# Layer 0 of a four-layer graph network: where the first scores stand in VectorE's queue

## The chip, the cores and the metric

The kernel runs on one core of a Trainium2 chip. The metric is the device time of one launch in microseconds (us), the median of several runs. Before the change it is 1615.28 us (three runs, 1614.99 to 1616.41).

The five engines each have a queue of their own and take it in order: TensorE (PE in the profile; PEld is its weight load), VectorE (DVE), ScalarE (ACT), GpSimd (POOL) and SyncE (SP). SP issues most of the loads, ACT the stores, and POOL the gathers by index. An engine whose next instruction waits for a semaphore does nothing of what stands behind it.

## The reference

Four graph-attention layers run one after the other on `x` (4096 rows of 256 numbers), all with the same 0/1 matrix `adj` (4096 x 4096). `adj` is sparse: a row has a few neighbours and itself. Layer 0 is the one that the change touches:

```
h = maximum(layernorm(x), 0) @ W.T                 # 8 heads of 32
e_l, e_r = sums of h * a_l and h * a_r per head
logits = leaky_relu(e_l[i] + e_r[j], 0.2) + gate * sum_f |curv[i,f] - curv[j,f]| * Wc[h,f]
attn = softmax over the j with adj[i,j] > 0
x = x + sum_j attn[i,j] * h[j]
```

The layers 1, 2 and 3 have other scores, and the same pattern of neighbours.

## The kernel before, in words

The kernel never forms the 4096 x 4096 scores. It finds for each tile of 128 rows the list of columns that hold an edge, gathers the rows of those columns from a table in device memory, and works on the gathered rows. There are 32 tiles (`NT`), numbered t; nine gathers (`EC`) of 128 rows each serve one tile. The gathered rows of a tile are its buffer `g`, of which there are six (`G = 6`).

Layer 0 does two jobs at once. **Finding**: `piece` loads `adj` in 128 pieces of 512 KB through SP and turns each into a mask (on ACT, a few on VectorE); `pack` multiplies the masks on TensorE into keys; sixteen pieces make the keys of one group of four tiles. `rank` takes the largest keys of a tile on VectorE (three MAX8 and two MATCH_REPLACE8), `columns` turns the keys of a group into column numbers (some thirty small VectorE instructions), `places` works out where each edge goes (four matmuls with `degree`, then some eighteen VectorE instructions, the last of which, line 1415, writes `both`), `mark` makes the 0/1 matrix `st` of a tile, and `find_edges` multiplies it on TensorE and ends in line 1466, which writes `nbr`, the indices of the tile's nine gathers. **Attending**: `begin0` and `begin0_late` issue the nine gathers of a tile on POOL and a load of its own rows on SP (line 927), `before0` makes `pb` and `s_f` on TensorE and ACT, `score0` forms `d` (line 1505) and `e` (1507, 1508) from `g` and `pb` on VectorE, `turn_d` and `curve` take `d` through TensorE (1512, 1518), `weigh0` scales the gathered rows (1531, the longest VectorE instruction of the layer), `attend0` sums them on TensorE (934 to 943), `finish0`, `turn1` and `rows1` add the result to `x` and make the row of layer 1's table. `attend0` of a tile frees its `g`, which the gathers of the tile six later need.

The order is set in two ways. `put(when, f, ...)` gives every step of every tile a planned time; the steps are traced in the order of these times. TensorE's queue keeps that order exactly. The other queues are ordered by a scheduler that takes the traced order as priority and puts an instruction where its model of the machine has the inputs ready. `found[t]` is the planned time at which a tile's list is known, `begun[t]` the planned time of its gathers, `w` the time from which the steps after them are counted: `before0` at w - 10, `score0` at w - 9, `turn_d` at w - 7.8, `curve` at w + 2, `weigh0` at w + 3, `attend0` at w + 15. With this problem's sizes `begun[t]` is 91 + 11.5 t, so `w` is 113 + 11.5 t, and the group that holds the tiles 4 to 7 is ranked at 92.5 to 100, has `columns` at 101, `places` at 119 and its first `find_edges` at 127.

`tc.issue_after(i)` is a block: an instruction traced in it stands behind instruction i in the queue of i's engine. It is an order and not a semaphore. Layer 1 and 2 use it already: `scores` (line 1760) goes behind what the dictionary `behind` holds.

Of the kernel before, what the change touches and what calls it, by code (L numbers as in the profile page):

```python
# [21 lines left out]
C = 256  # L22
KC = C // P
H0, D0, CF = 8, 32, 6
# [672 lines left out]
EC = 9  # L697
# [16 lines left out]
def gnn_lists(  # L714
# [27 lines left out]
    nc = tc.nc  # L742
# [88 lines left out]
    behind = {}  # L831
# [23 lines left out]
    def bank(pool, name, dtype=F32):  # L855
        t = pool.tile([P, 512], F32, name=name)
        return t if dtype == F32 else t.bitcast(dtype)
# [96 lines left out]
    with tc.tile_pool(name="keep", bufs=1) as keep, tc.tile_pool(  # L954
# [9 lines left out]
        g = g_pool.tile([P, EC + 1, ROW0], F32, name="g").rearrange("p c k -> p (c k)")  # L964
# [44 lines left out]
        for i, size in enumerate((0.5, 1.0)):  # L1009
            d = keep.tile([P, P], BF16, name=f"off_diag{i}")  # L1010
# [218 lines left out]
        def rank(t):  # L1229

            r, i = divmod(t, RG // P)
            src = bank(ps_t, "pt")[:, : NH * KP]
            for h in range(NH):
                nc.tensor.transpose(
                    src[:, h * KP : (h + 1) * KP], key_t[r, h][:KP, i * P : (i + 1) * P], ident[:KP, :KP]
                )
            left = find.tile([P, NH * KP], F32, name="left", bufs=1)
            for a in range(0, KMAX, 8):
                best = keys[:, t, a : a + 8]
                nc.vector.max(out=best, in_=src)  # L1240
                if a + 8 < KMAX:
                    nc.vector.match_replace(out=left, in_to_replace=best, in_values=src, imm_value=-1.0)
                    src = left
# [65 lines left out]
        lists = {}  # L1309
# [54 lines left out]
        def places(q, n):  # L1364


            s = slice(q, q + n)
            K = KMAX + KX
            is_, lasts, both = lists.pop(q)
            ps = bank(ps_t, "pt")[:, : 4 * n].rearrange("p (a t) -> p a t", a=4)  # L1370
            nc.tensor.matmul(ps[:, 0, :], lhsT=below, rhs=degree[:, s, 0], start=True, stop=True)
            nc.tensor.matmul(ps[:, 1, :], lhsT=up_to, rhs=degree[:, s, 1], start=True, stop=True)
            for i in range(2):
                nc.tensor.matmul(ps[:, 2 + i, :], lhsT=ones, rhs=degree[:, s, i], start=True, stop=True)

            def tmp(name, *shape):
                return find.tile([P, GT, *shape], F32, name=name, bufs=1)[:, :n]


            end, first, step = tmp("end"), tmp("first", 2), tmp("step", 2)  # L1380
            nc.vector.tensor_scalar(end, ps[:, 3, :], -1.0, float(HALF), op0=OP.mult, op1=OP.add)
            nc.vector.tensor_scalar(
                end, end, float(LATE * P - HALF), second, op0=OP.min, op1=OP.mult
            )
            nc.vector.scalar_tensor_tensor(
                at[:, s], ps[:, 0, :], room, end, op0=OP.add, op1=OP.add
            )
            nc.vector.tensor_scalar(at_late[:, s], ps[:, 1, :], float(HALF), None, op0=OP.add)
            nc.scalar.copy(of_tile[:, s, :], ps[:, 2:, :].rearrange("p a t -> p t a"))
            for i, a in enumerate((at, at_late)):  # L1390
                nc.vector.scalar_tensor_tensor(
                    minus[:, s, i], a[:, s], -2.0, degree[:, s, i], op0=OP.mult, op1=OP.subtract
                )


            nc.vector.tensor_sub(first[:, :, 0], at[:, s], lasts[:, :, 1])
            nc.vector.tensor_sub(step[:, :, 0], at_late[:, s], first[:, :, 0])
            nc.vector.tensor_sub(step[:, :, 1], lasts[:, :, 0], degree[:, s, 1])
            nc.vector.tensor_add(first[:, :, 1], at[:, s], step[:, :, 1])
            nc.vector.tensor_sub(step[:, :, 1], at_late[:, s], first[:, :, 1])  # L1400
            nc.vector.tensor_add(step[:, :, 1], step[:, :, 1], lasts[:, :, 1])
            place_, late = tmp("place_", K), is_[:, :, 1, :]
            for i, (a, b) in enumerate(((0, KMAX), (KMAX, K))):
                shape = [P, n, b - a]
                nc.vector.tensor_tensor(
                    late[:, :, a:b], late[:, :, a:b], step[:, :, i : i + 1].to_broadcast(shape),
                    op=OP.mult,
                )
                nc.vector.tensor_tensor(
                    place_[:, :, a:b], first[:, :, i : i + 1].to_broadcast(shape),  # L1410
                    slot[:, None, a:b].to_broadcast(shape), op=OP.add,
                )
            nc.vector.tensor_add(place_, place_, late)

            nc.vector.scalar_tensor_tensor(
                both[:, :, 0, :], is_[:, :, 0, :], float(FAR), place_, op0=OP.mult, op1=OP.add
            )
            for i in range(n):
                of0[q + i]["list"] = both[:, i]

        def fits():

            every = slice(0, NT)

            def tmp(name):
                return find.tile([P, NT], F32, name=name, bufs=1)

            fails(every, keys[:, :, KMAX - 1], 0.0)
            fails(every, more[:, :, 7], 0.0)
            fails(every, at, from_, OP.is_lt)  # L1430
            fails(every, at_late, floor, OP.is_lt)
            end, over, any_ = tmp("end_"), tmp("over"), tmp("any_")
            nc.vector.tensor_add(end, at, degree[:, :, 0])
            fails(every, end, to)
            fails(every, of_tile[:, :, 0], float(LATE * P))
            nc.vector.tensor_add(over, of_tile[:, :, 0], of_tile[:, :, 1])
            fails(every, over, float(EC * P))
            nc.vector.tensor_add(any_, degree[:, :, 0], degree[:, :, 1])
            nc.vector.tensor_add(any_, any_, loop)
            fails(every, any_, 0.5, OP.is_lt)  # L1440
# [60 lines left out]
        def score0(t):  # L1501
            g = of0[t]["g"]
            pe = of0[t]["b"][:, : (EC + 1) * V0].rearrange("p (c k) -> p c k", c=EC + 1)
            d = of0[t]["d"] = work.tile([P, EC, CF], F32, name="d")
            nc.vector.tensor_sub(d, g[:, :EC, C + H0 :], pe[:, :EC, H0:])  # L1505
            e = of0[t]["e"] = work.tile([P, EC + 1, H0], F32, name="e")
            nc.vector.tensor_add(e, g[:, :, C : C + H0], pe[:, :, :H0])
            nc.vector.scalar_tensor_tensor(e, e, 0.2, e, op0=OP.mult, op1=OP.max)
# [58 lines left out]
        def put(when, f, *a):  # L1567
            plan.append((when, len(plan), f, a))
# [5 lines left out]
        def at_piece(i):  # L1574
            return 8 + T_PIECE * min(i, FIRST) + T_LATER * max(i - FIRST, 0)
# [15 lines left out]
        for q, n in groups:  # L1591
            for t in range(q, q + n):
                last = at_piece((t // (RG // P) + 1) * per_r - 1) + 7 + 2.5 * (t % (RG // P))
                put(last, rank, t)
            put(last + 1, columns, q, n)
            put(last + 19, places, q, n)
            for t in range(q, q + n):
                found[t] = last + 23
        first = 17 + NE // P * T_ROWS
        begun = {}  # L1600
# [3 lines left out]
            put(when, mark, t)  # L1604
            put(when + 4, find_edges, t)
        for t in range(NT):
            w = begun[t] + 22
            put(begun[t], begin0, t)
            put(max(begun[t] + 0.1, begun[0] + 12), begin0_late, t)
            put(w - 10, before0, t)  # L1610
            put(w - 9 + 0, score0, t)
            put(w - 7.8 + 0, turn_d, t)
            put(w + 2, curve, t)
            put(w + 3, weigh0, t)
            put(w + 15, attend0, t)
            put(w + 20, finish0, t)
            put(w + 24.6, turn1, t)
            put(w + 27, rows1, t)
        put(found[NT - 1] + 20, fits)
        for _, _, f, a in sorted(plan, key=lambda p: p[:2]):  # L1620
            f(*a)
        bad_1 = const.tile([P, 1], F32, name="bad_1")
        nc.vector.tensor_reduce(bad_1, bad, AX.X, OP.add)

# [489 lines left out]
def gnn_kernel(tc: tile.TileContext, a: dict, out: bass.AP):  # L2114

    nc = tc.nc
    with tc.tile_pool(name="result", bufs=1, space=DRAM) as result:
        misfit = result.tile([1, 1], I32, name="misfit")
        gnn_lists(
            tc, *(a[k] for k in LISTS_TAKE), out, misfit,  # L2120
        )
        flag = nc.values_load(misfit[0:1, 0:1], min_val=0, max_val=1 << 20, skip_runtime_bounds_check_because="a count of rows")
        with tc.If(flag > 0):
            gnn_dense(tc, *(a[k] for k in DENSE_TAKE), out)
# [70 lines left out]
```

## Time and profile before

One profiled execution took 2274.1 us, with a span of 2272.3 us from its first to its last instruction; the median of the runs without a profile is 1615.28 us.

| stretch of the span, us | what runs | PE busy | DVE busy | ACT busy | POOL busy | granted TensorE clock | DMA share |
|---|---|---|---|---|---|---|---|
| 0 to 108 | finding, table of layer 0 | 66.6 | 65.8 | 59.1 | 16.3 | 0.94 | 0.88 |
| 108 to 440 | finding and attending | 161.6 | 154.8 | 139.9 | 137.6 | 0.63 | 0.58 |
| 440 to 780 | the same; the last pieces of `adj` | 208.7 | 168.6 | 121.2 | 137.4 | 0.69 | 0.45 |
| 780 to 860 | from layer 0 to layer 1 | 31.6 | 26.7 | 21.1 | 45.6 | 0.66 | 0.52 |
| 860 to 1340 | layer 1 | 281.4 | 180.6 | 103.6 | 234.7 | 0.74 | 0.46 |
| 1340 to 1850 | layer 2 | 375.3 | 233.3 | 160.0 | 284.8 | 0.86 | 0.51 |
| 1850 to 2272 | layer 3 | 306.0 | 270.5 | 160.3 | 197.8 | 0.88 | 0.41 |

Busy times are us within the stretch. No engine fills a stretch, so what sets the pace is a chain of waits, and the table alone doesn't name it. POOL's busy time is nearly all gathers, 1088 of them in the four layers (288, 256, 288 and 256).

### The profile page before, as it was taken

The numbers are of one execution on the slowest core, as the hardware profiler recorded it, in microseconds if no ns is written. First come the engines' busy times: TensorE is split into PE (matmuls) and PEld (weight loads), VectorE is DVE, ScalarE is ACT, GpSimd is POOL, SyncE is SP. The second block draws the span as 40 slices with busy tenths as digits, with TensorE's granted clock in tenths as the row PEclk, the third lists the DMA queues.
The fourth block names the chain that finished last, engine by engine and source line by source line (L and its number), as shares of the span: only waits on it lengthen the run. The fifth ranks groups of instructions, "written<-read, shape, count | busy, mean of one in ns | idle before, by whom it ended". The sixth has DMA issues, their size and how long they took to land.

```text
span 2272.3 us, 28902 instructions
## 1 busy us (share of the span) xinstructions
PE 1431.2 (63%) x9569; PEld 1013.5 (45%) x9584; DVE 1100.3 (48%) x2979; ACT 765.2 (34%) x2246; POOL 1054.0 (46%) x1145
## 2 busy tenths in 40 slices
PE   5723745656646726656556637878889367767776
PEld 3412423333434414434444425666667345445544
DVE  5724635555543524434333323554555256666666
ACT  4623624454222322222222102333334143343343
POOL 2154243443344354454444455666562635565550
PEclk9855766666666857777777858999999778898888
DMA  8855555665333354444444444555554444455530
GB/s 284 267 187 172 187 172 180 212 212 163 83 88 99 88 164 130 128 124 129 130 133 131 140 138 122 158 161 157 155 156 139 129 134 147 149 157 154 161 107 21
DMA packets 167341, 338.02 MB, mean 149 GB/s; under 512 B 31760, under 2 KB 103696, under 8 KB 167184
## 3 DMA queue, kind: packets, MB, share of 16 engines
q0 software_dynamic: 52224, 145.30, 24.5%
q1 hardware_dynamic: 67714, 134.54, 18.1%
q10 hardware_dynamic: 47246, 56.27, 7.1%
q8 instruction: 77, 1.26, 0.2%
q14 instruction: 80, 0.66, 0.1%
HBM read 282.22 MB, written 53.77 MB: 148 GB/s over the span
## 4 chain that ended last, share of the span: by engine, by line
PE 25%; issue 12%; DVE 9%; another core or an unknown queue 8%; ACT 3%; POOL 1%; DMA 1%; DVEq 0%; ACTq 0%; POOLq 0%
PE o L934 5%; PE o L1894 4%; PE o L939 4%; PE pv L2025 3%; PE pt L872 3%; DVE v L2031 2%; PE pt L1929 2%; PE o L943 1%; POOL g L914 1%; DVE s L2052 1%; PE s_ps L1641 1%; DMA g<-table,nbr 1%; PE pe L1674 1%; DVE g L2064 1%
## 5 line engine op out<-in xcount | busy, mean ns | idle before, releaser
L914 POOL DMA_INDIRECT g<-table,nbr x1088 | 1037.8, 954 | 1065.1 <-issue 433.9
L1894 PE MATMUL o<-g,sw 128*128 128x257 f32 x896 | 206.0, 388 | 31.2 <-DVE sw L1872 23.6
L1894 PEld LDWEIGHTS o<-g,sw 128*128 128x128 f32 x896 | 173.1, 194 | 59.7 <-issue 25.3
L863 PE MATMUL pt<-ident,r 128*128 128x128 f32 x256 | 61.9, 328 | 193.4 <-DVE r L843 60.4
L2025 PE MATMUL pv<-parts,st 64*128 64x256 bf16 (+1 forms) x864 | 106.3, 308 | 97.8 <-DVE v L2031 42.0
L2031 DVE TENSOR_TENSOR v<-pv,g 128x512 f32<-128x512 f32 (+1 forms) x160 | 97.3, 634 | 89.6 <-remote 51.2
L863 PEld LDWEIGHTS pt<-ident,r 128*128 128x128 f32 x256 | 34.4, 162 | 219.2 <-issue 115.4
L1192 ACT ACTIVATE mask<-adj,minus_half 128x1024 bf16<-128x1024 int32 x112 | 125.2, 1141 | 18.1 <-issue 6.8
L934 PE MATMUL o<-g,sw 128*128 128x257 f32 (+1 forms) x320 | 125.5, 544 | 0.0
L865 ACT COPY hT<-pt 128x256 f32<-128x256 f32 x128 | 46.9, 367 | 233.4 <-PE pt L863 144.3
L872 PE MATMUL pt<-wcat,hT 128*128 128x272 f32 (+2 forms) x384 | 96.7, 371 | 45.3 <-ACT hT L865 32.4
L1674 PE MATMUL pe<-ident,col_late 128*128 128x128 f32 x64 | 23.3, 463 | 158.2 <-issue 144.8
L2025 PEld LDWEIGHTS <-st 64*128 64x128 bf16 (+1 forms) x864 | 61.4, 104 | 136.6 <-issue 125.9
L2081 ACT ACTIVATE y<-o,inv 128x64 f32<-128x64 f32 x128 | 36.0, 312 | 243.4 <-DVE inv L2077 143.5
L939 PE MATMUL o<-g,sw 128*64 128x257 f32 (+1 forms) x768 | 117.3, 448 | 0.0
L896 ACT ACTIVATE off<-place,minus 128x1152 bf16<-128x1152 f16 x64 | 80.0, 1250 | 58.1 <-DVE st L897 53.0
L1505 DVE TENSOR_TENSOR d<-g,pb 128x54 f32<-128x54 f32 x32 | 6.8, 211 | 180.1 <-remote 124.9
L934 PEld LDWEIGHTS o<-g,sw 128*128 128x128 f32 x320 | 85.8, 279 | 18.1 <-DVE g L2064 0.3
L872 PEld LDWEIGHTS pt<-wcat,hT 128*128 128x128 f32 x384 | 66.1, 208 | 60.2 <-ACT hT L865 36.5
L1531 DVE TENSOR_TENSOR g<-g,pb 128x2560 f32<-128x2560 f32 x32 | 90.1, 2816 | 4.7 <-ACT pb L1528 4.4
L1674 PEld LDWEIGHTS pe<-ident,col_late 128*128 128x128 f32 x64 | 14.7, 285 | 168.3 <-issue 153.1
L1688 PEld LDWEIGHTS <-st 128*128 128x128 bf16 x768 | 76.7, 105 | 19.4 <-issue 8.6
(363 smaller groups left out, 3028.5 us busy)
## 6 DMA issues: line engine op xcount, KB each, us to landing
adj<-in_adj_l SPq DMA_DIRECT2D x128, 512.0 KB
g<-table,nbr POOLq DMA_INDIRECT x1088
rows_of<-st ACTq DMA_DIRECT2D x16, 832.0 KB
st<-rows_of SPq DMA_DIRECT2D x16, 832.0 KB
x<-x SPq DMA_DIRECT2D x24, 512.0 KB
st<-rows_of SPq DMA_DIRECT2D x16, 576.0 KB
table<-row ACTq DMA_DIRECT2D x32, 258.0 KB
g<-table SPq DMA_DIRECT2D x64, 129.0 KB
```

What stands on the lines that cost most here:

```text
L863: nc.tensor.transpose(pt[:, k, :], h[:, k * P : (k + 1) * P], ident)
L872: nc.tensor.matmul(pp, lhsT=hT[:, k, :], rhs=w[:, k, :], start=(k == 0), stop=(k == KC - 1))
L896: nc.scalar.activation(off, place, AF.Abs, bias=minus[:, t, 0:1], scale=1.0)
L914: nc.gpsimd.indirect_dma_start(out=g[:, c, :width], out_offset=None, in_=table[: NE if c < EARLY else N, :], in_offset=bass.IndirectOffset ...
L934: nc.tensor.matmul(o, lhsT=a, rhs=b, start=(i == 0), stop=False)
L939: nc.tensor.matmul(o[rows], lhsT=s[:, c + h * HC, rows], rhs=g[:, c + h * HC, :width], start=False, stop=False,)
L1192: nc.scalar.activation(m, a, AF.Sign, bias=minus_half, scale=1.0)
L1531: nc.vector.tensor_mul(gh, gh, w[:, :, :, None].to_broadcast([P, K, H0, D0]))
L1688: nc.tensor.matmul(ps, lhsT=to[:, b * P : (b + 1) * P], rhs=late_rows[:, b, i, :width], start=(b == 0 and i == 0), stop=(b == LB - 1 and i ...
L1894: nc.tensor.matmul(o, lhsT=sw[:, h, i].rearrange("p s r -> p (s r)"), rhs=g[:, c, : C + 1], start=(i == 0), stop=(i == HC + 1),)
L2025: nc.tensor.matmul(to, lhsT=st[r, c * P : (c + 1) * P], rhs=parts[r, i, :], start=(i == 0), stop=(i == 2),)
L2031: nc.vector.tensor_mul(v[:, chunks, :], pv, g[:, chunks, :C])
```

## The change

`behind["lists"]` keeps the newest instruction of the finding that was traced: the MAX8 of `rank`, or the last instruction of `places`. In the first two tiles of every group of four, the first instruction of `score0`, the subtraction that writes `d`, is traced in a block behind that instruction. The bound `t < 32` holds for every tile. The two other instructions of `score0` get no order of their own. `w` becomes the larger of its old value and 121 + 8 t, which differs for the tiles 0, 1 and 2 alone: 121, 129 and 137 in place of 113, 124.5 and 136. Since every step from `before0` to `rows1` is counted from `w`, these steps of the three tiles are traced later by 8, 4.5 and 1 planned us; the gathers are not. At the end of layer 0 the entry is taken out of `behind`, so that `scores` of the layers 1 and 2 doesn't see it.

```
-                nc.vector.max(out=best, in_=src)
+                behind["lists"] = nc.vector.max(out=best, in_=src)
...
-            nc.vector.scalar_tensor_tensor(
+            last = nc.vector.scalar_tensor_tensor(
                 both[:, :, 0, :], is_[:, :, 0, :], float(FAR), place_, op0=OP.mult, op1=OP.add
             )
             for i in range(n):
                 of0[q + i]["list"] = both[:, i]
+            behind["lists"] = last
...
-            nc.vector.tensor_sub(d, g[:, :EC, C + H0 :], pe[:, :EC, H0:])
+            with ExitStack() as queue:
+                if t < 32 and t % 4 < 2:
+                    queue.enter_context(tc.issue_after(behind["lists"].ins))
+                nc.vector.tensor_sub(d, g[:, :EC, C + H0 :], pe[:, :EC, H0:])
...
-            w = begun[t] + 22
+            w = max(begun[t] + 22, begun[0] + 30 + 8 * t)
...
         for _, _, f, a in sorted(plan, key=lambda p: p[:2]):
             f(*a)
+        behind.pop("lists")
```

No computation is added or removed.

## The prediction

> **What bounds the kernel now.** I read five views in this order: the page's costliest groups, the timeline of POOL, the view of line 1505, the timeline of VectorE around it, and the waits of TensorE.
>
> ```profile
> L914 POOL DMA_INDIRECT g<-table,nbr x1088 | 1037.8, 954 | 1065.1 <-issue 433.9
> L1505 DVE TENSOR_TENSOR d<-g,pb 128x54 f32<-128x54 f32 x32 | 6.8, 211 | 180.1 <-remote 124.9
> ```
>
> The gathers are one group of 1088, and VectorE stood idle 180.1 us in front of `d`. Next POOL's own order of time, about the first four tiles:
>
> ```profile
> 108.44 1.19 POOL L914 DMA_INDIRECT g<-table,nbr  x1 [4.30 <-DVE nbr L1466]
> 109.93 0.95 POOL L914 DMA_INDIRECT g<-table,nbr  x1 [0.30 <-issue]
> ...
> 152.45 0.94 POOL L914 DMA_INDIRECT g<-table,nbr  x1 [0.30 <-issue]
> 185.43 0.94 POOL L914 DMA_INDIRECT g<-table,nbr  x1 [32.04 <-DVE nbr L1466]
> ```
>
> 36 gathers run from 108.44 to 152.45, one per 1.257 us; then POOL idles 32.04 us for tile 4's `nbr`, made by VectorE. What VectorE did meanwhile:
>
> ```profile
> 118.63 0.43 DVE L1240 MAX8 keys<-left 128x8 f32<-128x256 f32 x1
> 159.38 0.21 DVE L1505 TENSOR_TENSOR d<-g,pb 128x54 f32<-128x54 f32 x1 [40.32 <-remote]
> ...
> 165.50 0.21 DVE L1505 TENSOR_TENSOR d<-g,pb 128x54 f32<-128x54 f32 x1 [0.42 <-PE pb L1490]
> ...
> 168.79 2.82 DVE L1531 TENSOR_TENSOR g<-g,pb 128x2560 f32<-128x2560 f32 x1
> ...
> 178.26 0.21 DVE L1505 TENSOR_TENSOR d<-g,pb 128x54 f32<-128x54 f32 x1
> ...
> 184.99 0.17 DVE L1466 TENSOR_SCALAR nbr<-to_col 128x9 uint32<-128x9 f32 x1
> ```
>
> It waited 40.32 us with tile 0's `d` at its head, in the middle of ranking tiles 4 to 7. But not for the gather: the view of line 1505 in this window has the four waits for the gather queues in front of that `d`,
>
> ```profile
> L1505 DVEq EVENT_SEMAPHORE  x4: 49/50/939, 120.7 to 124.0; - x4
> ```
>
> the last done by 124.9; the rest of the wait is for TensorE's `pb`. And TensorE limped:
>
> ```profile
> PE pb L1486 <- issue: 66.7, 79, 3.3
> PE pt L1498 <- issue: 57.1, 62, 2.6
> ```
>
> It stalls for no recorded reason behind bursts of 27 small matmuls (`before0`). The profiled execution is 658.8 us longer than the median (2274.1 - 1615.3), so I take most of these stalls as the profile's own. This is the decisive choice: **of the 40 us only the part up to 124.9, some 6 us, is taken to exist in timed runs.**
>
> What then bounds timed runs? 1088 gathers at 1.257 us are 1368 us; from 108.4 they end at 1476. That leaves 1615 - 1476 = 139 us for everything else: the tail (66 us from the last gather at 2206.1 to the end at 2272.3 in the trace), three changes of layer, and all idle time. So POOL must be the pace in timed runs, layer 0 can hide only a few tens of us of idle, and the change gains only where it removes idle time of POOL.
>
> **What the Trainium skill says.** "Perfetto Trace Analysis", section "Per-instruction lifecycle": an instruction of VectorE waits for its semaphores in a wait queue, outside the reported window. The trace agrees: `d` reads 211 ns, and its cost is the 40.32 us ahead of it. "DMA: Bandwidth & Descriptors", section "SWDGE vs HWDGE vs iDMA": GpSimd's software descriptors have one queue. The trace agrees, gathers never overlap on POOL. "NOTIFIC — the notification-queue block", section 7.1: the block that writes trace records can hold back an engine when its own pipeline fills. That fits the `issue` stalls; no run here proves it yet.
>
> **The change part by part.** First, before, in timed terms. Deadline: POOL wants tile 4's `nbr` at 108.4 + 36 x 1.257 = 153.7, tile 5's at 165.0, tile 6's at 176.3. Chain: `d` of tile 0 at 124.9. From there the trace needs 6.1 us to `d` of tile 1 (165.50 - 159.38), 131.0; but that tile's gathers are issued until 130.9, and the DMA records end at 132.4: wait 1.4. Then 12.8 us to `d` of tile 2 (145.2; its gathers land at 143.6) and 6.7 us to `nbr`: **151.9, slack 1.8 us.** Tile 5: 13.9 us later in the trace (198.88), of which 5.6 is idle "issue": about 160, slack 5.
>
> Removed from that chain: (a) the order of VectorE's queue, which a build shows, puts tile 0's `d` behind the remaining rank instructions, one `key_t` and one cast. They took 159.51 to 163.22, less 0.6 for `d` and `e` between them: 3.1 us that now run inside the wait. (b) `d` of tile 1 goes behind `places`, where its gather has long landed: 1.4 us. (c) `weigh0` of tile 1, 2.8 us (a row like 168.79), falls behind tile 5's `nbr`; tile 0's stays ahead of tile 4's. (d) The `places` matmuls precede `turn_d` of tile 1 on TensorE: under 0.5 us. Sum about 7.3: **tile 4's `nbr` at 145**, tile 5's near 150, because its `find_edges` no longer follows `attend0` of tile 0 (184.09 to 189.70 on TensorE, 5.6 us).
>
> Added: no semaphore, only order. Behind tile 1's `d` stand its `e`, marks and `nbr` of 4; `places` needs TensorE but no gather, so the wait is for work that is ready. Moved later: `attend0` of tile 0 goes behind `find_edges` of 4 to 7 on TensorE, some 8 us by the plan, more if ranking of the next group is late; tile 6's gathers need its buffer at 176.3. From 145 or 150 plus 5.6 that is met with about 15 us to spare. SP: the load of tile 6's own rows, which waits for the same buffer, stands behind 59 `adj` pieces instead of 55, so four pieces pass it; the next stands behind 63 instead of 61. Nothing else moves there by more than a few places. Later groups: `d` of tiles 12, 13, 17, 20 and 21 moves behind `places` or `mark` by a few instructions, 1 to 4 us each. In the plan lists run 8 + 6 us per group ahead of the gathers, so these count nothing. From layer 1 on the order is the same.
>
> The gain is therefore how much before misses its deadline, capped at about 7 us for tile 4. My slack of 1.8 comes from a chain that crosses engines five times; a miss of 5 to 8 us is as easy as a hit. Bound below: 0. Bound above: 32.04 us of idle POOL if timed runs stall as the profile did. I take **5 us: 1615.3 - 5 = 1610.3**. In the profile's own terms, if the TensorE stalls repeat, `d` of tile 0 still waits until about 159 and the gain is 7 of 2274.
>
> **The rivals.**
> No change: the deadline is met already. For it: slack 1.8 and POOL's closed sum. Against: 139 us of rest is more than the tail. Time 1615, within 3.2.
> A larger gain: VectorE's wait for TensorE is real without the profile too, and several groups stall. For it: the row of line 1505 puts 124.9 of its 180.1 us down to "remote", not to gathers. Against: the 659 us. Two or three holds of 5 to 10 us: 1595.
> Slower: attention of tiles 0 to 2 now stands on TensorE behind the ranking of the third group (tiles 8 to 11), which needs `adj` pieces up to 48. If those keys come after about 165, `attend0` of tile 0 ends after 176 and POOL waits for the buffer; SP stops behind tile 6's own rows with the pieces from 60 on unissued, and finding falls back in turn. Price: one us per us beyond 176; with keys 15 us late, 10 us: 1625. Against: the plan has those keys 20 us earlier. For it: in the trace POOL does wait for buffers, tile 7's gathers by 9.9 us (`nbr` 225.1, issue 235.0).
>
> **How the numbers follow.** A measurement tells about 0.2%, 3.2 us, from no change. Forecast (gain of 3 to 12) 0.32, larger gain 0.10, no change 0.26, slower 0.32, the last raised because so tight a queue order has many places to lose. Faster 0.42, same 0.26, slower 0.32. Range 1598 to 1630: it cuts half of the large gains (0.05) and the slower cases with finding stopped twice (0.11). The forecast's own range is 1603 to 1612.
>
> **What would show it.** In the new profile: tile 0's `d` after the last MAX8 of tile 7; `places` of the second group before tile 1's `d`; POOL's gap ahead of gather 37 shorter than 32.04 by about 7; `attend0` of tile 0 behind four `find_edges`. Wrong if that gap closes altogether, if gathers of tiles 6 and 7 wait longer for `attend0`, or if SP stalls longer at line 927.

## The result, and the profile after

The change makes no difference that can be measured. Recorded with it: 1616.69 us median of four runs against 1615.62, ratio 1.0005 (95% interval 0.9988 to 1.0022). A later comparison of 22 runs with 27 gave 1614.21 against 1615.85, ratio 0.9996 (0.9986 to 1.0005), so the change is worth between 2.3 us saved and 0.8 lost.

One thing has to be said ahead of all numbers. On two of the chips before takes about 2277 us in place of 1615, and every trace taken there shows TensorE standing still after bursts of small matmuls; the profile shown ahead of the prediction (2274.1 us) is of this kind. The profiled execution of after took 1615.86 us (span 1614.1), like its other runs, so for a fair comparison I took two more traces of before on a chip that gives 1615. The first five experiments fell on the two stalling chips and are compared among themselves alone.

After, the costliest group of the page and TensorE's waits at the lines of `before0`:

```profile
L914 POOL DMA_INDIRECT g<-table,nbr x1088 | 1046.0, 961 | 400.0 <-issue 305.2
```

```profile
PE pb L1487 <- DVE g L1535: 3.0, 1, 3.0
PE pt L1499 <- DVE left L1242: 1.6, 3, 0.6
```

POOL's idle time is 400.0 us, not 1065.1, and the 66.7 and 57.1 us of `issue` stalls in `before0` are gone. The change did not remove them: the new trace of before (span 1614.5) has 404.3 us and no such stall either.

```profile
L914 POOL DMA_INDIRECT g<-table,nbr x1088 | 1044.2, 960 | 404.3 <-issue 310.3
```

VectorE's order of time around the first `d`, first in this trace of before:

```profile
120.37 0.43 DVE L1240 MAX8 keys<-left 128x8 f32<-128x256 f32 x1
126.79 0.21 DVE L1505 TENSOR_TENSOR d<-g,pb 128x54 f32<-128x54 f32 x1 [6.00 <-DMA g<-table,nbr]
...
137.76 0.21 DVE L1505 TENSOR_TENSOR d<-g,pb 128x54 f32<-128x54 f32 x1 [5.10 <-DMA g<-table,nbr]
...
157.00 0.17 DVE L1466 TENSOR_SCALAR nbr<-to_col 128x9 uint32<-128x9 f32 x1
```

and the same stretch of after:

```profile
125.22 0.43 DVE L1240 MAX8 keys<-left 128x8 f32<-128x256 f32 x1
128.26 0.75 DVE L1225 SCALAR_TENSOR_TENSOR key_t<-some,seg_of,kps 128x512 f32<-128x512 f32 x1 [2.61 <-ACT some L1223]
...
129.41 0.21 DVE L1509 TENSOR_TENSOR d<-g,pb 128x54 f32<-128x54 f32 x1 [0.28 <-issue]
...
139.10 0.16 DVE L1398 TENSOR_TENSOR step<-lasts,degree 128x4 f32<-128x4 f32 x1 [2.08 <-ACT degree L1356]
...
143.03 0.29 DVE L1415 SCALAR_TENSOR_TENSOR both<-is__1600,place__1765 128x128 f16<-128x128 f32 x1
143.43 0.21 DVE L1509 TENSOR_TENSOR d<-g,pb 128x54 f32<-128x54 f32 x1
...
145.47 0.23 DVE L1530 TENSOR_TENSOR e<-e,pb 128x72 f32<-128x72 f32 x1 [1.10 <-PE pb L1522]
...
151.55 0.17 DVE L1467 TENSOR_SCALAR nbr<-to_col 128x9 uint32<-128x9 f32 x1
```

The reader is to see three things. Before had two waits for gathers at the head of VectorE's queue, 6.00 and 5.10 us. After has neither: tile 0's `d` comes behind the last MAX8, tile 1's behind line 1415. And part of the saving goes to waits that were hidden until then, for ACT and TensorE (2.61, 2.08, 1.10; in the second trace of after 2.54, 1.11 and 1.11, and 1.75 in front of tile 2's `d`). From tile 3's `nbr` to tile 4's the windows of the two traces read (us; busy times of PE, PEld, DVE, ACT, POOL with their instructions, granted clock, DMA share, GB/s):

```profile
116.90:157.00 40.10, 17.28 (x183) 11.13 (x183) 25.12 (x92) 23.46 (x33) 30.09 (x31) 0.50 0.94 332
```

```profile
118.80:151.50 32.70, 16.34 (x180) 9.98 (x178) 23.68 (x90) 23.45 (x32) 24.88 (x26) 0.50 1.00 354
```

The stretch is 7.4 us shorter: VectorE has 1.4 us less to do in it (work moved behind `nbr`), and idles 9.0 us in place of 15.0.

So the list of tile 4 comes 7.4 us earlier. What did it buy? POOL's gaps in front of tiles 4, 8, 12 and 16 of before:

```profile
157.44 0.94 POOL L914 DMA_INDIRECT g<-table,nbr  x1 [1.30 <-DVE nbr L1466]
211.44 0.94 POOL L914 DMA_INDIRECT g<-table,nbr  x1 [8.09 <-ACT mask L1192]
263.86 0.94 POOL L914 DMA_INDIRECT g<-table,nbr  x1 [6.86 <-ACT mask L1192]
311.84 0.94 POOL L914 DMA_INDIRECT g<-table,nbr  x1 [2.18 <-DMA table<-row]
```

and of after:

```profile
157.85 0.95 POOL L914 DMA_INDIRECT g<-table,nbr  x1 [0.30 <-issue]
...
207.03 0.94 POOL L914 DMA_INDIRECT g<-table,nbr  x1 [3.38 <-ACT mask L1192]
259.48 0.94 POOL L914 DMA_INDIRECT g<-table,nbr  x1 [6.23 <-ACT mask L1192]
307.06 0.94 POOL L914 DMA_INDIRECT g<-table,nbr  x1 [1.43 <-DMA table<-row]
```

0.30 us is the usual pause between two gathers. Before was late for tile 4 by 1.0 us (1.30 - 0.30), and that is gone; larger gaps stand in front of tiles 8 and 12 in both. The releaser named there is the nearest recorded event, not the cause. In after VectorE starts to write tile 8's list 1.0 us ahead of the gather, and in all these traces the gathers of tiles 8, 12 and 16 that had a gap start 0.83 us after their list is written:

```profile
206.03 0.17 DVE L1467 TENSOR_SCALAR nbr<-to_col 128x9 uint32<-128x9 f32 x1
```

Further on in layer 0 the lists are no longer what POOL waits for. From tile 18 on they are 4 to 10 us early, and each gather with a gap of over 1 us starts 0.75 us after the last matmul of the `attend0` that frees its buffer, six tiles back; so it is in after with tile 20's, behind tile 14's `attend0`:

```profile
358.46 0.71 PE L943 MATMUL o<-g,s_f 128*128 128x264 f32 x2
```

```profile
359.92 0.94 POOL L914 DMA_INDIRECT g<-table,nbr  x1 [5.50 <-issue]
```

These gaps, less the usual pauses, add up to 22.5 us in before and 22.7 in after, while those for lists (tiles 4, 8, 12 and 16) fall from 17.2 to 10.1.

The time of tile 0's list varies by execution, from 107.4 to 112.7 us in my runs, whatever the kernel. Counted from that list, the traces of one kernel agree within 1.2 us (us; "list" is the start of `nbr`; the last row is the end of the span; the four right-hand columns are experiments below):

| | before, two traces | after, two traces | order alone | 12 us late | 26 gathers fewer | lighter product |
|---|---|---|---|---|---|---|
| list of tile 4 | 47.3, 47.8 | 40.0, 40.1 | 47.4 | 54.5 | 39.8 | 41.8 |
| list of tile 8 | 100.7, 101.3 | 94.4, 94.7 | 100.0 | 108.3 | 97.2 | 88.8 |
| list of tile 12 | 153.2, 153.7 | 146.9, 147.3 | 150.8 | 160.8 | 149.8 | 137.6 |
| list of tile 16 | 201.1, 201.4 | 194.5, 194.9 | 198.4 | 208.8 | 197.6 | 186.1 |
| first gather, layer 1 | 411.9, 412.6 | 407.3, 408.5 | 411.1 | 421.4 | 410.6 | 381.0 |
| first gather, layer 2 | 741.9, 742.4 | 738.1, 739.3 | 741.7 | 752.5 | 741.3 | 710.8 |
| first gather, layer 3 | 1106.4, 1107.2 | 1102.3, 1103.3 | 1105.8 | 1117.0 | 1105.4 | 1074.5 |
| end | 1504.8, 1505.3 | 1502.5, 1503.0 | 1506.0 | 1516.6 | 1512.3 | 1473.8 |

The change does what it says, and the lists of tiles 4, 8, 12 and 16 gain 6 to 8 us by it. At the start of layer 1 some 4.4 us are left, at the end 2.3, which is 0.14% and inside what the timed runs can't tell from nothing.

### The profile page after: what moved, and what is told of

Same layout as the page of the kernel before. It is cut to its first block, busy times and chain, and to the rows that moved or that the text cites. A ratio compares the mean times of both kernels' runs of the same rounds, so it can differ in the third digit from the quotient of the medians.

```text
span 1614.1 us, 28920 instructions
## 1 busy us (share of the span) xinstructions
PE 1272.5 (79%) x9584; PEld 928.0 (57%) x9584; DVE 1088.7 (67%) x2978; ACT 765.1 (47%) x2247; POOL 1061.5 (66%) x1145
## 4 chain that ended last, share of the span: by engine, by line
PE 46%; POOL 12%; DMA 11%; DVE 9%; issue 9%; ACT 6%; ACTq 0%; DVEq 0%; POOLq 0%; SPq 0%
PE o L1899 12%; POOL g L914 12%; DMA g<-table,nbr 10%; PE o L934 8%; PE o L939 6%; PE pt L1934 3%; PE pv L2030 3%; PE pt L872 3%; PE o L943 3%; DVE v L2036 2%; PE pt L863 1%; PE s_ps L1646 1%; PE pe L1693 1%; ACT mask L1192 1%; ACT s_f L1500 1%
## 5 line engine op out<-in xcount | busy, mean ns | idle before, releaser
L1899 PEld LDWEIGHTS o<-g,sw 128*128 128x128 f32 x896 | 170.4, 190 | 62.7 <-DVE sw L1877 36.3
L2030 PE MATMUL pv<-parts,st 64*128 64x256 bf16 (+1 forms) x864 | 94.1, 288 | 67.9 <-DVE v L2036 65.9
L939 PE MATMUL o<-g,sw 128*64 128x257 f32 (+1 forms) x768 | 101.6, 401 | 0.0
L1646 PE MATMUL s_ps<-ident_b,st 128*128 128x128 bf16 x864 | 67.8, 227 | 37.5 <-DVE sw L1795 37.2
L863 PE MATMUL pt<-ident,r 128*128 128x128 f32 x256 | 56.0, 305 | 47.9 <-DVE r L843 19.6
L934 PE MATMUL o<-g,sw 128*128 128x257 f32 (+1 forms) x320 | 92.3, 424 | 0.0
L1535 DVE TENSOR_TENSOR g<-g,pb 128x2560 f32<-128x2560 f32 x32 | 90.1, 2816 | 2.2 <-ACT pb L1532 1.9
L2069 DVE TENSOR_TENSOR g<-g,pm 128x2048 f32<-128x2048 f32 x32 | 73.2, 2289 | 25.8 <-ACT pm L2062 25.8
L1693 PEld LDWEIGHTS <-st 128*128 128x128 bf16 x768 | 79.0, 108 | 14.3 <-issue 1.6
L1646 PEld LDWEIGHTS <-st 128*128 128x128 bf16 x864 | 57.7, 101 | 47.6 <-DVE sw L1795 29.4
L2057 DVE TENSOR_REDUCE s<-v 128x36 f32<-128x2304 f32 x32 | 81.7, 2553 | 1.1
L1500 ACT CAST s_f<-pt 128x1024 f32<-128x1024 bf16 x64 | 37.7, 641 | 90.3 <-PE o L943 90.3
```

Source lines behind the costliest of these rows:

```text
L934: nc.tensor.matmul(o, lhsT=a, rhs=b, start=(i == 0), stop=False)
L939: nc.tensor.matmul(o[rows], lhsT=s[:, c + h * HC, rows], rhs=g[:, c + h * HC, :width], start=False, stop=False,)
L1535: nc.vector.tensor_mul(gh, gh, w[:, :, :, None].to_broadcast([P, K, H0, D0]))
L1646: nc.tensor.transpose(pt[:, c, :], st[:, c * P : (c + 1) * P], ident_b)
L1693: nc.tensor.matmul(ps, lhsT=to[:, b * P : (b + 1) * P], rhs=late_rows[:, b, i, :width], start=(b == 0 and i == 0), stop=(b == LB - 1 and i ...
L1899: nc.tensor.matmul(o, lhsT=sw[:, h, i].rearrange("p s r -> p (s r)"), rhs=g[:, c, : C + 1], start=(i == 0), stop=(i == HC + 1),)
```

## The experiments

**Before and the two parts on a stalling chip.** `before_look` is before, unchanged.

> The kernel before, unchanged, for a second profiled execution to read beside that of after. Theory A (the first group's lists meet POOL's deadline already): the wait of the first d ends near 125 to 129 us as in after, nbr of tile 4 comes before POOL has issued tile 3's last gather (about 157), and POOL has no gap of over 1 us in front of gather 37. Theory B (the lists were late and the gain was given back later): a gap of 3 to 8 us stands there, and it is missing in after, with as much more idle time of POOL between tiles 8 and 20 in after. Both expect a span near 1614 us, not 2272.

`w_alone` is before with the later due times alone; `order_alone` is after with this line turned back, so that it has the order alone:

```
-            w = begun[t] + 22
+            w = max(begun[t] + 22, begun[0] + 30 + 8 * t)
```

> Only the later due times of the work of tiles 0 to 2, without the queue order of d. Theory A: 1615, ratio 1.000. Theory B (gain given back by the later attention): the loss without the gain, 1618 to 1622, ratio 1.002 to 1.004.

> Only the order of d behind the lists on VectorE, with the old due times. Theory A: 1615, ratio 1.000. Theory B: the gain without the loss, 1609 to 1612, ratio 0.996 to 0.998.

The chip took 2277 us for before. `before_look` repeated the profile shown ahead of the prediction, with VectorE's wait of 40.3 us in front of the first `d` and a gap of 31.7 us beyond the usual pause in front of gather 37. `before_again` was to bring a trace near 1615 us and missed that: on another chip, it gave 2273 us and the same 31.7.

> The kernel before once more, for a trace of an execution near 1615 us (the last four runs, on a chip where TensorE stands still after bursts of small matmuls, took 2270 to 2290). Theory A: first d by 129 us, nbr of tile 4 before 157, no gap over 1 us in front of gather 37. Theory B: a gap of 3 to 8 us there.

Ratios there: `w_alone` 0.996 (0.9933 to 0.9986), `order_alone` 0.9989 (0.9961 to 1.0018). The wait for TensorE outlives the later due times:

```profile
DVE d L1505 <- remote: 35.4, 1, 35.4
```

So where TensorE stalls, the due times help a little (with them the gap in front of gather 37 is 26.6 us in place of 32.0) and for the order alone no gain is seen. Neither theory had foreseen this setting, and it says nothing on the runs near 1615 us. After once more, and two more traces of before, then came from a chip that gives 1615:

> The changed kernel, unchanged, beside before on one chip. Where before takes 1615: 1615 to 1617, ratio 1.000, as recorded (Theory A, POOL's deadline was met). Where TensorE stands still after bursts and before takes about 2277: if the two parts add up, w_alone's 0.996 and order_alone's 1.000 give 0.996, about 2268. If the wait of VectorE for TensorE in front of the first d is what the change takes away there (the rival of a larger gain), 0.990 or less, 2255.

> The kernel before, for a trace of an execution near 1615 us, where TensorE does not stand still after bursts. Theory A (POOL's deadline was met before the change): first d by 129 us, nbr of tile 4 before POOL has issued tile 3's gathers (about 155 to 157), no gap over 1.5 us in front of gather 37, and gaps of about 3 and 7 us in front of tiles 8 and 12 as in after. Theory B (gain at the first group, swallowed later): a gap of 3 to 8 us in front of gather 37 and smaller ones than after's in front of tiles 8 and 12.

> A second trace of before near 1615 us, to tell what repeats from what one execution happens to have. If the later lists are a property of the kernel: nbr of tiles 8, 12 and 16 at 210 +- 1.5, 262.5 +- 1.5 and 310.5 +- 1.5, first gather of layer 1 at 521 +- 1. If they were chance: within 1.5 us of after's two traces (204 to 206, 256.5 to 258.5, 304 to 306; 517.7 to 518.9).

`after_again` gave the 0.9996 above. `before_third` (1616.17 us) and `before_fourth` (1619.72 us) are the two columns of the table. The first `d` ended its wait by 126.8 us as Theory A had it, but the gap in front of gather 37 is neither nothing nor 3 to 8 us: 1.0 and 1.6. The gaps in front of tiles 8 and 12 are larger than after's (lines above), where Theory B had them smaller. The later lists are a property of the kernel: measured from tile 0's list they repeat within 0.6 us. In absolute time `before_fourth` missed my bands (214.0 for tile 8), as its whole execution began 3 us late.

**VectorE 12 us later.** In after, the finding of tile 4 gets 28 superfluous MAX8 ahead of its list:

```
             to_col = find.tile([P, EC], F32, name="to_col")
+            for _ in range(28 if t == 4 else 0):
+                nc.vector.max(out=to_col[:, :8], in_=near.rearrange("p c k -> p (c k)")[:, :256])
             nc.vector.tensor_reduce(to_col, near, AX.X, OP.min)
```

> After, with 28 more MAX8 of 128x256 (about 0.43 us each, 12 us) on VectorE right ahead of tile 4's nbr, which in after comes at 151.5 us, 5.3 us ahead of need (POOL is free for tile 4 at 157.8 and a list needs 1.0 us to be taken up, as nbr of tile 8 at 206.0 and its gather at 207.0 show). A gap of about 7 us opens in front of gather 37. Theory A1 (POOL's pace: each us of idle POOL costs one): 1622 to 1624. Theory A2 (VectorE's whole work up to about 430 us sets the length of layer 0): 1627 to 1629. Theory A3 (something later waits in any case, the lists of tiles 8 and 12 for the mask's pieces or the buffers from tile 17 on, and swallows the gap): 1615 to 1618, with the gaps in front of tiles 8 and 12, now 3.3 and 7.3 us, smaller.

That first try met a stalling chip: ratio 1.0027 (0.9998 to 1.0057) against before, from which nothing on POOL's deadline follows. Again, on a chip that gives 1615:

> After with 28 more MAX8 of 128x256 (12 us) on VectorE ahead of tile 4's nbr. Where before takes 1615: a gap of about 7 us opens in front of gather 37 (slack 5.3 us). Theory A1 (POOL's pace, each us of idle POOL costs one): ratio 1.004, 1621 to 1623. Theory A2 (VectorE's whole work sets the length of layer 0): 1.0075, 1627. Theory A3 (what stands in front of tiles 8, 12 and from 17 on swallows it): 0.999 to 1.001.

1625.77 us, ratio 1.0059 (1.0042 to 1.0076), 9 to 12 us above after's two medians. POOL's gaps in front of tiles 4, 8, 12 and 16:

```profile
162.75 0.94 POOL L914 DMA_INDIRECT g<-table,nbr  x1 [8.64 <-DVE nbr L1469]
217.05 0.95 POOL L914 DMA_INDIRECT g<-table,nbr  x1 [8.86 <-ACT mask L1192]
269.58 0.94 POOL L914 DMA_INDIRECT g<-table,nbr  x1 [7.38 <-ACT mask L1192]
317.54 0.94 POOL L914 DMA_INDIRECT g<-table,nbr  x1 [2.97 <-DMA table<-row]
```

The gap in front of tile 4 is 8.3 us, and the loss is larger: the gaps behind it do not shrink to swallow it, as A3 wanted, they grow too. By the table all lists move by 13 to 15 us, and so does the end (1516.6 against 1502.8). That is VectorE's whole extra time and about 1 us more (20 of the 28 took 9.21 us in the trace, so 12.9), not the part that POOL idled. Its theory A2 had 1627, A1 1622; the measurement lies between, and the trace speaks for A2.

**Is POOL the pace?** One experiment takes time from POOL, one from VectorE, both on after. In the first the tiles from 6 on gather eight times in layer 0 and load their own rows in place of the first gather:

```
-            of0[t]["g"] = gather_early(t, table0, ROW0, g_pool)
+            of0[t]["g"] = gather_early(t, table0, ROW0, g_pool, t >= G)
...
+            if t >= G:
+                nc.sync.dma_start(of0[t]["g"][:, 0, :ROW0], tile_rows(table0, t))
```

> After, where in layer 0 tiles 6 to 31 leave out the first of their nine gathers, and load the tile's own rows in its place on SyncE's queue (same bytes): 26 gathers, 33 us of POOL's time less. Theory A1 (POOL's pace sets layer 0): 1614 - 33 = 1581 to 1585, ratio 0.980. Theory A2 or A3 (POOL waits for lists and buffers between tiles 8 and 24, and is the pace for the last 8 tiles alone): 8 to 12 us of gain, 1602 to 1607, ratio 0.993 to 0.995, with longer waits of POOL for buffers.

In the second, VectorE's longest instruction of the layer covers one column in ten and leaves out the other nine:

```
-            nc.vector.tensor_mul(gh, gh, w[:, :, :, None].to_broadcast([P, K, H0, D0]))
+            nc.vector.tensor_mul(gh[:, :1], gh[:, :1], w[:, :1, :, None].to_broadcast([P, 1, H0, D0]))
```

> After, where the product of the gathered rows with their weights in layer 0 covers one of ten columns of edges (9/10 of this product left out): 32 instructions of 2.82 us on VectorE become about 0.3 us, 80 us less. Theory A2 (VectorE's work sets the length up to about 430 us, POOL's pace behind that): the waits of POOL for lists and buffers close, some 20 to 30 us of gain, 1585 to 1595, ratio 0.982 to 0.988. Theory A1: only the wait in front of the buffers, under 8 us, 1607 to 1615. Theory A3 with the mask's pieces as the stop: 5 us or less.

Without 33 us of gathers the time rose: 1620.76 us, ratio 1.0033 (1.0020 to 1.0046). The time that POOL no longer works, it waits, in front of tiles 8, 12 and 16:

```profile
208.78 0.94 POOL L914 DMA_INDIRECT g<-table,nbr  x1 [8.06 <-ACT mask L1192]
261.37 0.95 POOL L914 DMA_INDIRECT g<-table,nbr  x1 [12.37 <-ACT mask L1192]
309.25 0.94 POOL L914 DMA_INDIRECT g<-table,nbr  x1 [7.12 <-ACT rstd L835]
```

The first two gaps and the third exceed after's by 4.7, 6.1 and 5.7 us. Even the gain of 8 to 12 us from the last eight tiles, which A2 and A3 had, didn't come: the gaps in front of the buffers grew too, from 22.7 us in after to 39.0, and layer 1 began no sooner (410.6 in the table, 2.8 us later than after's mean). The added loads on SP are not told apart from the left-out gathers. That the whole is longer still says nothing about layer 0: 6.4 us of it lie behind the last gather (1622.8 - 1553.7 = 69.1 us, in after 1614.1 - 1551.4 = 62.7), and all of these behind the branch at the very end of the program, where POOL's longest `DRAIN` takes 8.90 us, in after 2.36 (maximum of the three durations, ns):

```profile
L2199 POOLq DRAIN  x3: 40/107/8897, 1613.1 to 1622.6; - x3
```

```profile
L2197 POOLq DRAIN  x3: 40/107/2364, 1609.2 to 1613.9; - x3
```

Why it takes longer there is open.

With the lighter product the 32 instructions took 13.3 us in place of 90.1, which is 77 us less on VectorE and not the 80 expected. The time fell by 26.6 us against before: 1588.57 us, ratio 0.9825 (0.9803 to 0.9848). Tiles 8 and 12 find no gap:

```profile
205.45 0.94 POOL L914 DMA_INDIRECT g<-table,nbr  x1 [0.30 <-ACT hT L865]
...
250.87 1.02 POOL L914 DMA_INDIRECT g<-table,nbr  x1 [0.30 <-PE o L934]
...
299.33 0.95 POOL L914 DMA_INDIRECT g<-table,nbr  x1 [3.02 <-PE pt L1234]
```

POOL's idle time within the gathers of layer 0 falls from 41.6 us (112.1 to 512.4 less 287 x 1.25) to 18.1. From list to list (tile 4 to 8, 8 to 12, 12 to 16) it needs 47.0, 48.7 and 48.5 us; before 53.4, 52.5 and 47.9, after 54.5, 52.5 and 47.6. The gaps in front of the buffers fall from 22.7 us to 7.9. **Work on VectorE, and not POOL's, sets the rhythm: of the lists, which POOL waits for up to tile 16, and of the buffers, which it waits for from tile 18 on.** The change leaves this rhythm as it is and starts it 7 us sooner. Two other candidates are as busy as VectorE. From tile 4's list to tile 8's before reads (columns as above)

```profile
157.00:210.40 53.40, 41.41 (x405) 27.28 (x407) 42.02 (x142) 35.78 (x68) 35.24 (x36) 0.83 0.84 275
```

with 41.4 us of TensorE beside 42.0 of VectorE, and a DMA share of 0.84. But the lighter product takes no matmul and no transfer away, and the time fell. What is not told apart is VectorE's busy time and the length of the path through it: the lighter product, 2.4 us shorter for each tile, also shortens the way from a tile's gathers to the `attend0` that frees their buffer, and 18 of the 27 us by which layer 1 starts sooner than in after arise behind tile 16's list.

**The two parts near 1615 us.** `order_alone` again, on a chip that gives 1615:

> The order of d behind the lists with the old due times of tiles 0 to 2. Theory P (VectorE's dead waits of 6.0 and 5.1 us for gathers in front of the first two d are what delays all the lists of layer 0, the order takes them away, and what remains of it at the start of layer 1 is passed on to the end): lists of tiles 8, 12 and 16 at 204 to 206, 256 to 258.5 and 304 to 306 as in after, ratio as after's, 0.9985 to 1.000. Theory Q (the later due times give some of it back): lists as early, 0.996 to 0.998, 1609 to 1612. Theory R (the due times are what brings the gain in layer 0): lists as late as before's, 1.000 or over.

1618.12 us, ratio 1.0026 (1.0009 to 1.0043): Theory R, though the lists of tiles 12 and 16 come 2.6 and 2.9 us sooner than before's. The order alone thus costs some 4 us in the timed runs, of which its trace shows 1.0 at the end (1506.0 against 1505.0). VectorE's waits up to tile 4's list are

```profile
DVE d L1509 <- DMA g<-table,nbr: 10.7, 2, 7.7
DVE end L1381 <- PE pt L1374: 1.8, 1, 1.8
```

and before had 11.1 us in two such waits. The wait in front of tile 0's `d` shrinks to 3.0 us, and the one of tile 1 grows to 7.7:

```profile
125.02 0.21 DVE L1509 TENSOR_TENSOR d<-g,pb 128x54 f32<-128x54 f32 x1 [2.97 <-DMA g<-table,nbr]
...
136.23 0.21 DVE L1509 TENSOR_TENSOR d<-g,pb 128x54 f32<-128x54 f32 x1 [7.74 <-DMA g<-table,nbr]
```

With the old due times tile 1's `score0` is traced ahead of `places`, so that the entry it follows is still the MAX8 of `rank`. The later due times make it follow `places`; only with them does the order take both waits away. Whether they alone would do it near 1615 us was not tried.

## Why the prediction was right or wrong

The measured medians, 1616.69 and 1614.21 us, lie in the range of 1598 to 1630, but outside the forecast's own 1603 to 1612: the most likely outcome was said to be faster (0.42), and no change had 0.26. The change does to the queues what was foreseen. What this is worth was reasoned from the wrong pace, and the time fell into the range by the range's width more than by the reasoning.

- **"Of the 40 us only some 6 us exist in timed runs"**: right for the runs that count, 6.00 us, ending at 126.8 where I had 124.9. The reason was not: the stalls are no matter of the profile as such, since on two chips the runs all take about 2277 us, and on a third the executions profiled in the same way have no stalls. What the Trainium skill says of the trace writer in section 7.1 of "NOTIFIC — the notification-queue block" is not shown by any run to be the cause, which stays open.
- **The chain to tile 4**: I had 151.9 before, 145 after, 7 us apart. Measured 157.0 and 151.6 or 149.4, and 7.5 apart counted from tile 0's list. The sum held by two errors that cancel: tile 1's gathers landed at 137.1, not 132.4, so that term (b) was a wait of 5.10 us and not 1.4; and against it stand the waits of 2.61, 2.08 and 1.10 us that came up, of which I had said nothing. That the sum came to 7.3 and the measurement to 7.5 is luck.
- **POOL's deadline**: slack 1.8 us by my sum, a miss of 1.0 to 1.6 measured. By POOL's pause alone the gain would have been that and no more. In after the gap in front of gather 37 closed altogether, which I had named as a sign of being wrong; but that sign was written for a gap of 32.04 us, and before's on a like chip is 1.30 and 1.93.
- **"In the plan lists run 8 + 6 us per group ahead of the gathers, so these count nothing"**: wrong, and with it "POOL must be the pace". The plan's times are no measurement. POOL stands idle 7.8, 6.6 and 1.9 us for the lists of tiles 8, 12 and 16 in before and 22.5 for buffers behind them, and taking 33 us from POOL gained nothing, while 77 us from VectorE gained 26.6. And the gain at tile 4 wasn't capped by its gap but reached all groups (6.4 at tile 8, 6.6 at tile 16, 5.7 at the last list).
- **The gain of 5 us**: reached at the start of layer 1 (4.4 between the means of the traces), not at the end (2.3), and not seen in the timed runs. The step that failed is the one that I didn't write down, that a gain of layer 0 is passed on whole. At the change of layer some of it is lost where tile 27's row, the last that layer 1's first gathers read, is stored (ACT's queue): 9.7 us after its last matmul of `attend0` in before (507.8), 11.4 in after (503.9). ACT waits 4.39 us in after, 2.76 in before, in front of the cast to `s_f` that stands ahead of this row in its queue; the second traces have 4.40 and 2.76.

```profile
517.52 0.38 ACTq L774 DMA_DIRECT2D table<-row  x1
```

```profile
515.28 0.38 ACTq L774 DMA_DIRECT2D table<-row  x1
```

  About 1 us each goes in layer 1, where the order of the queues is the same, and behind the last gather. The latter lies behind the branch that ends the program: from its load of `misfit` to the end both traces of before need 6.3 us, those of after 7.4 and 7.2. Why is open for both. It is no general loss: against after, the 26.9 us of the lighter product at the start of layer 1 are 29.0 at the end, and the 13.6 of the delay 13.8.
- **"No change" came for another reason than its own**: the deadline was not met; the gain was there and shrank under what can be told.
- **The slower rival**: `attend0` of tile 0 goes behind the four `find_edges`, as foreseen (TensorE in after),

```profile
162.74 0.42 PE L1453 MATMUL pt<-edge,ident_b 128*128 128x288 f16 x1 [1.90 <-DVE left L1242]
162.96 0.69 PE L1456 MATMUL pt<-both,st 128*128 128x32 f16 x18
163.49 1.23 PE L934 MATMUL o<-g,ident 128*128 128x264 f32 x2
```

  and ends at 168.9, well ahead of tile 6's gathers at 181.0. SP's waits at line 927 (from 100 to 520 us, the three releasers named most) add up to 102.5 and 88.9 us in the two traces of before, 97.2 and 103.1 in those of after, which shows no clear loss. I had given this rival 0.32; tile 6's and 7's gathers wait for no buffer in either trace of after.

## What to carry to other kernels

Before a dead wait is priced, find out which engine's work sets the rhythm behind it: here leaving work out on POOL gained nothing and leaving it out on VectorE gained a third of it, which two runs showed and the share of busy time (66% and 67%) didn't. Look along the whole layer, too: POOL waited for lists in its first half and for buffers in its second. A wait taken away at the head of a queue starts the rhythm sooner once; it doesn't shorten it, and hidden waits of 1 to 3 us come up in its place. Times by which a plan runs ahead are no slack until a trace shows the gap.

## What was not expected of the hardware

The same kernel takes 1615 us on one chip and about 2277 us on two others, steadily, without any difference in its instructions: in the three traces of before at 2277 us TensorE's waits of kind `issue` at the two lines of `before0` are 57 to 68 us each, and 128 to 145 at line 1674; in those at 1615 there are none at these lines. This is under half of the 660 us; the rest was not followed up. And of the 3.5 us between the two traces of before near 1615 us, 3.0 are there at the first list (109.7 and 112.7 us after the start); counted from that list the traces of one kernel repeat within about 1 us, so that two traces each show a difference of 2 us that 49 timed runs only hint at.
